# Second attention's row scores by way of a line in DRAM, in a two-layer graph kernel

## The chip, the cores and the metric

The kernel runs on one core of a Trainium2 chip. The metric is the device time of one execution in microseconds. Before the change the median of three runs is 2951.56 us (2950.34 to 2952.9).

## The reference

The input is 64 graphs of 256 nodes with 256 features, and a 0/1 adjacency matrix for each. The first layer applies graph attention twice, adds the input, normalises, and ends with a feed-forward block. The second layer is an eight-head attention in which the adjacency picks the value matrix, with a feed-forward block of its own. The change is in the second of the two graph attentions:

```python
def _gat(h, adj, W, a, out_features):
    Wh = jnp.matmul(h, W)
    Wh1 = jnp.matmul(Wh, a[:out_features])
    Wh2 = jnp.matmul(Wh, a[out_features:])
    e = Wh1 + jnp.swapaxes(Wh2, 1, 2)
    e = jax.nn.leaky_relu(e, negative_slope=ALPHA)
    scores = jnp.where(adj > 0, e, NEG)
    att = jax.nn.softmax(scores, axis=1)
    return jnp.matmul(att, Wh)
...
h = _gat(x, adj, W1, a1, Fout)
h = _gat(h, adj, W2, a2, W2.shape[1])
```

Each score is the sum of a number of one node and a number of the other. So a tile of scores needs one of the two vectors down the partitions (a column) and the other along the free axis, the same in all partitions (the rows).

## The kernel before, in words

Two graphs make a group; there are 32 groups. A group's 512 nodes are four blocks of 128 (T = 4). After a start that is written out by hand for groups 0 and 1, the kernel works in turns (`turn`, L1275). In turn u it carries three groups at once: Y = u through the second layer, X = u + 1 through the first layer's feed-forward block, and Z = u + 2 through the two graph attentions. The 30 turns u = 0 to 29 have a Z; the last two have none.

Within a turn the order on TensorE, SP, VectorE and ScalarE is the order of the program text (`manual_schedule`, L1323 to L1325). GpSimd's order, and the way in which one turn's VectorE and ScalarE work interleaves with the next turn's, is left to a planner. Engines wait for each other through semaphores.

The part of a turn around the change, in program order:

- `first_sums(z, ...)` (L1530, L1535): TensorE multiplies the first attention's weights with the values, and ScalarE copies the result to `hp` (L841), 260 columns wide, of which 258 are written. The first 256 columns are the second attention's values, column F = 256 the number for the rows, column F + 1 the number for the columns.
- `hidden_seven` (L908) for Y: the first matmul of the second layer's feed-forward block in seven products of half size instead of eight ("2a" to "4b", the letter names one half of the outputs). VectorE and ScalarE gather the products in `h` (L947, L950), and ScalarE applies the activation (L956). Laid between these steps is X's norm: moments (L865), GpSimd's power (L877), ScalarE's and GpSimd's normalising (L894, L891), the affine step for Y (L903, L906), and `normed_features` (L712), which transposes 32x32 blocks on VectorE (L717) and moves them to their places with 12 DMAs on SP (L726, `hT<-yt`) and 4 copies on GpSimd.
- `second_scores(z)` (L1588): `score_rows` (L777) makes the rows. For each of the four blocks TensorE transposes column F of `hp`, spread over 128 columns, into a PSUM bank (L781), so that every partition holds the same line. `Softmax.raw` (L797, L799) adds the column number to it on ScalarE, 256 elements at a time; `leaky` (L807) follows on VectorE, then `exp` (L810), `masks` (L814), the reciprocal (L818) and `scaled` (L830).
- `HiddenOut` (L997) for Y: the feed-forward block's second matmul, again in seven products. Product 1 reads `h`. Product 5 reads the quarter sum s1 = a21 + a22, which `out.sums(1, 2)` makes on VectorE (L1013, tile `eq`); `out.add` adds the products to `y` (L1035). Then TensorE applies the second attention's weights (`second_sums`, L1206, tile `ygp`).

```python
            second_scores(z)
            out = HiddenOut(y_, 1, y, h1, w2s, out_sums(y_, 1))
            out.product(1)
            out.sums(1, 2)
            Z["m"].scores(0)
            out.add(1)
            out.product(5)
            Z["m"].scores(1)
```

On SP's queue, ahead of the 12 moves, stand the store of the group before (L1243) and the load of the next group's rows `y` (L441); behind them come the 8 loads of the next adjacency (L449), and the moves for Y's and X's other norms (L737). The pool tag `es` has two buffers; `node_sums` (L1131) and `reciprocals` (L1149) take them. PSUM has a tag `g` with six banks, which the rows share with the products.

Of the kernel before, what the change touches and what calls it, by code (L numbers as in the profile page):

```python
# [9 lines left out]
F32 = mybir.dt.float32  # L10
# [6 lines left out]
P = 128  # L17
# [368 lines left out]
def narrow_path(  # L386
# [13 lines left out]
    nc = tc.nc  # L400
    B, N, F = x.shape
# [7 lines left out]
    T = G * NB  # L409
    TN = G * N  # L410
# [6 lines left out]
    const = ctx.enter_context(tc.tile_pool(name="const", bufs=1))  # L417
    io = ctx.enter_context(tc.tile_pool(name="io", bufs=2))
    work = ctx.enter_context(tc.tile_pool(name="work", bufs=2))
    psum = ctx.enter_context(tc.tile_pool(name="psum", bufs=1, space=PSUM))  # L420
    ctx.enter_context(nc.allow_non_contiguous_dma(reason="vectors, once"))

    def bank(name):
        return psum.tile([P, 512], F32, tag="g", name=name, bufs=6)
# [258 lines left out]
    rows = work.tile([P, T, 2 * F], F32, tag="v", name="rows", bufs=1)  # L683
# [93 lines left out]
    def score_rows(u, l, wh, c):  # L777

        rows = bank(f"rows{u}_{l}")
        for t in range(T):  # L780
            nc.tensor.transpose(rows[:, t * P:(t + 1) * P],  # L781
                                wh[:, t, c:c + 1].to_broadcast([P, P]), ident)
        return rows

    class Softmax:
# [46 lines left out]
    def gat_first(u, s, xp, hp=None, blocks=range(T)):  # L832
        if hp is None:
            hp = work.tile([P, T, WX], F32, tag="wh", name=f"hp{u}")
        for t in blocks:
            b, i = divmod(t, NB)
            ps = bank(f"hpp{u}_{t}")
            for j in range(NB):
                nc.tensor.matmul(ps[:, :WH], s[:, b * NB + j, i * P:(i + 1) * P],  # L839
                                 xp[:, b * NB + j, :WH], start=(j == 0), stop=(j == NB - 1))  # L840
            nc.scalar.copy(hp[:, t, :WH], ps[:, :WH])  # L841
        return hp
# [199 lines left out]
    def out_sums(u, l):  # L1042
        two = [work.tile([P, HPB, NB * N], F32, tag=t, name=f"{t}q{u}_{l}") for t in ("e", "ea")]
        return [t[:, :, i * N:(i + 1) * N] for t in two for i in range(2)]
# [136 lines left out]
        d = g[z]  # L1181
        d["xp"] = projected(z, d["xT"], blocks, d.get("xp"))

    def first_scores(z):
        d = g[z]
        d["m"] = Softmax(z, 0, d["xp"], score_rows(z, 0, d["xp"], F + 2), F + 3)

    def second_scores(z):
        d = g[z]
        d["m"] = Softmax(z, 1, d["hp"], score_rows(z, 1, d["hp"], F), F + 1)  # L1190

    def first_softmax(z):
        first_scores(z)
        g[z]["m"].all()
        g[z]["m"].scaled(WH)

    def second_softmax(z):
        second_scores(z)
        g[z]["m"].all()
        g[z]["m"].scaled(F)  # L1200

    def first_sums(z, blocks=range(T)):
        d = g[z]
        d["hp"] = gat_first(z, d["m"].s, d["xp"], None if blocks[0] == 0 else d["hp"], blocks)
# [70 lines left out]
    def turn(y_, x_, z, rest=None):  # L1275
        Y, X, Z = (g.get(u) for u in (y_, x_, z))
        hT, y = Y["hT"], Y["y"]
        quads = [(b, m) for b in range(G) for m in range(KB)]
        p = Projections(y_, hT)
# [45 lines left out]
        with order:  # L1325
# [151 lines left out]
            if Z:  # L1477
                first_scores(z)
# [54 lines left out]
                n = moments(x_, 1, X["y"], range(NB))  # L1533
            if Z:
                first_sums(z, range(T // 2, T))  # L1535
            if X:
                out.product(4)
            tt = work.tile([P, HPB, NB * N], F32, tag="e", name=f"tt{y_}_1")
# [39 lines left out]
            if y_ >= NG - 2:  # L1578
# [5 lines left out]
                else:  # L1584
                    for _ in pieces:
                        pass
                return
            second_scores(z)  # L1588
            out = HiddenOut(y_, 1, y, h1, w2s, out_sums(y_, 1))
            out.product(1)  # L1590
            out.sums(1, 2)
# [26 lines left out]
    with tc.manual_schedule(engines={getattr(mybir.EngineType, n) for n in  # L1618
# [21 lines left out]
        turn_a = early_adjacency_of(0, 1)  # L1640
        turn_a()
        first_scores(0)
        shift_products(ps, wf1, range(4, FB), lb1)
        shift_added(ps, range(FB), bf1)
# [13 lines left out]
        scaled_rows(wqk, *pqk)  # L1658
        nc.vector.tensor_tensor(wv[:, :, 1, :], wv[:, :, 1, :], wv[:, :, 0, :], ALU.subtract)
        second_scores(0)  # L1660
        turn_b.append(early_adjacency_of(1, 1))
        spread(a["m"])
# [115 lines left out]
    with tc.manual_schedule(engines={mybir.EngineType.PE, mybir.EngineType.SP}):  # L1778
        for u in range(NG):
            turn(u, u + 1, u + 2, second_half)  # L1780


    c = work.tile([P, 4], F32, tag="mv", name="checks")
# [13 lines left out]
@with_exitstack  # L1797
def tile_gat_layer__then__relational_attention_layer(ctx: ExitStack, tc: tile.TileContext, *args):
    nc = tc.nc
    keep = ctx.enter_context(tc.tile_pool(name="keep", bufs=1))  # L1800
    bad = keep.tile([1, 1], I32, name="bad")
    narrow_path(tc, *args, bad)
    with tc.If(nc.values_load(bad[0:1, 0:1], min_val=0, max_val=P) > 0):
        general_path(tc, *args)
# [30 lines left out]
```

## Time and profile before

| | |
|---|---|
| Median of three runs | 2951.56 us |
| The profiled execution's own time | 2950.62 us |
| Its span, first to last instruction | 2949.0 us |
| TensorE matmul busy | 2921.7 us (99%) |
| VectorE busy | 2611.3 us (89%) |
| ScalarE busy | 1897.2 us (64%) |
| GpSimd busy | 625.6 us (21%) |
| Row transposes for the second attention (L781, `rows<-ident,hp`) | 128 of 273 ns (median) |
| ScalarE's additions on them (L799, `s<-rows,hp`) | 128 of 478 ns (median) |
| Granted TensorE clock | 0.998 |

PE is TensorE's matmul, PEld its weight load, which overlaps matmuls; DVE is VectorE, ACT ScalarE, POOL GpSimd, SPq the queue of SyncE that issues DMAs. In a timeline the columns are the start in us from the span's start, the duration in us, engine, line, operation, output and inputs, shapes and the number of instructions merged into one line. A bracket tells how long the engine was idle before it and what ended that. Matmuls overlap, so the distance between the starts tells more than the durations.

### The profile page before, as it was taken

The numbers are of one execution on the slowest core, as the hardware profiler recorded it, in microseconds if no ns is written. First come the engines' busy times: TensorE is split into PE (matmuls) and PEld (weight loads), VectorE is DVE, ScalarE is ACT, GpSimd is POOL, SyncE is SP. The second block draws the span as 40 slices with busy tenths as digits, with TensorE's granted clock in tenths as the row PEclk, the third lists the DMA queues.
The fourth block names the chain that finished last, engine by engine and source line by source line (L and its number), as shares of the span: only waits on it lengthen the run. The fifth ranks groups of instructions, "written<-read, shape, count | busy, mean of one in ns | idle before, by whom it ended". The sixth has DMA issues, their size and how long they took to land.

```text
span 2949.0 us, 58651 instructions
## 1 busy us (share of the span) xinstructions
PE 2921.7 (99%) x22206; PEld 2505.9 (85%) x22206; DVE 2611.3 (89%) x5028; ACT 1897.2 (64%) x3983; POOL 625.6 (21%) x931
## 2 busy tenths in 40 slices
PE   9999999999999999999999999999999999999997
PEld 7788888888888888888888888888888888888876
DVE  5889899989899889999898998899998989988887
ACT  5566666676676666666766766766667667667652
POOL 3312221122121122221221211222212212112211
PEclk9999999999999999999999999999999999999999
DMA  5011111111111111111111111111111111111000
GB/s 152 13 30 32 39 32 32 24 40 32 37 30 26 34 34 38 33 31 24 40 32 37 31 28 31 36 36 35 29 23 40 32 37 32 28 30 33 18 8 16
DMA packets 408020, 99.27 MB, mean 34 GB/s; under 512 B 357834, under 2 KB 407220, under 8 KB 407732
## 3 DMA queue, kind: packets, MB, share of 16 engines
q1 hardware_dynamic: 406332, 94.13, 14.8%
q8 instruction: 178, 2.92, 0.4%
q0 software_dynamic: 1056, 1.05, 0.1%
q14 instruction: 110, 0.90, 0.1%
q10 hardware_dynamic: 344, 0.28, 0.0%
HBM read 56.78 MB, written 16.78 MB: 25 GB/s over the span
## 4 chain that ended last, share of the span: by engine, by line
PE 97%; DVE 2%; ACT 1%; DMA 0%; issue 0%; POOL 0%; DVEq 0%; POOLq 0%; ACTq 0%
PE yf L1027 27%; PE h1a L938 15%; PE h1b L938 11%; PE po L1143 8%; PE v L1094 6%; PE qk L1094 6%; PE sp L1115 4%; PE hpp L839 4%; PE ygp L850 4%; PE xpp L772 4%; PE yop L850 4%; PE zo L1146 2%; PE rows L781 1%; DMA first<-in_adj_dram 0%; DVE st L865 0%
## 5 line engine op out<-in xcount | busy, mean ns | idle before, releaser
L1124 ACT ACTIVATE e<-sp 128x512 f32<-128x512 f32 x512 | 271.0, 611 | 71.2 <-issue 43.7
L1128 DVE TENSOR_TENSOR ea<-e,aT 128x1024 f32<-128x1024 f32 x256 | 311.1, 1217 | 1.6 <-ACT e L1124 1.6
L894 ACT ACTIVATE y<-y,nm,rs 128x256 f32<-128x256 f32 x442 | 235.1, 592 | 64.0 <-DVE nm L884 63.2
L947 DVE TENSOR_TENSOR h<-h1a,h 128x512 f32<-128x512 f32 x293 | 197.5, 682 | 81.7 <-PE h1a L938 78.5
L950 ACT COPY h<-h1b 128x512 f32<-128x512 f32 x293 | 175.2, 599 | 124.6 <-PE h1b L938 122.8
L956 ACT ACTIVATE h<-h,cols 128x256 f32<-128x256 f32 x512 | 221.9, 502 | 35.7 <-DVE h L947 31.5
L734 POOL COPY hT<-yt 32x256 f32<-32x256 f32 x244 | 211.3, 866 | 144.8 <-DVE yt L717 132.1
L1081 ACT COPY qk<-qk 128x512 f32<-128x512 f32 x128 | 74.3, 580 | 237.4 <-PE qk L1094 236.6
L865 DVE BATCH_NORM_STATS2 st<-y 128x6 f32<-128x256 f32 x512 | 208.7, 409 | 5.7
L876 POOL TENSOR_SCALAR rs<-mv 128x4 f32<-128x4 f32 (+1 forms) x134 | 41.7, 312 | 805.1 <-DVE mv L866 438.5
L1035 DVE TENSOR_TENSOR y<-yf,y 128x256 f32<-128x256 f32 x448 | 185.9, 415 | 29.8 <-PE yf L1027 29.8
L956 ACT ACTIVATE h<-h1a,cols 128x256 f32<-128x256 f32 x256 | 102.6, 465 | 131.9 <-PE h1a L938 131.9
L1156 POOL TENSOR_TENSOR low<-low,rq 128x16 f32<-128x16 f32 x64 | 13.9, 217 | 811.6 <-DVE rq L1155 811.6
L906 DVE TENSOR_TENSOR y<-y,rb 128x1024 f32<-128x1024 f32 x126 | 163.2, 1295 | 2.2
L1133 DVE TENSOR_TENSOR es<-e 128x1024 f32<-128x1024 f32 x128 | 156.0, 1219 | 0.0
L903 DVE TENSOR_TENSOR y<-y,rg 128x1024 f32<-128x1024 f32 x126 | 153.0, 1214 | 0.0
L877 POOL TENSOR_TENSOR rs<-rs,mhalf 128x4 f32<-128x4 f32 (+1 forms) x134 | 139.5, 1041 | 8.3
L1115 PE MATMUL sp<-qk 32*128 32x256 f32 x2048 | 138.4, 394 | 0.0
L938 PE MATMUL h1a<-tt,wf 128*128 128x256 f32 x512 | 137.7, 392 | 0.0
L1143 PE MATMUL po<-e,v 128*32 128x256 f32 x2048 | 135.5, 382 | 0.0
L1143 PE MATMUL po<-ea,v 128*32 128x256 f32 x2048 | 134.5, 379 | 0.0
L717 DVE STREAM_TRANSPOSE yt<-y 128x256 f32<-128x256 f32 x364 | 128.2, 407 | 0.9 <-ACT y L894 0.7
(288 smaller groups left out, 7738.4 us busy)
## 6 DMA issues: line engine op xcount, KB each, us to landing
hT<-yt SPq DMA_DIRECT2D x666, 32.0 KB, 1.8
y<-in_x_dram SPq DMA_DIRECT2D x32, 512.0 KB, 4.1
xq<-in_x_dram SPq DMA_DIRECT2D x240, 64.0 KB, 2.3
aq<-in_adj_dram SPq DMA_DIRECT2D x240, 64.0 KB, 2.3
out_dram<-y SPq DMA_DIRECT2D x30, 512.0 KB
wf<-in_L_gnn_w_ff_dram SPq DMA_DIRECT2D x2, 1024.0 KB, 7.8
w<-in_L_gnn_W_dram SPq DMA_DIRECT2D x2, 1024.0 KB
first<-in_adj_dram POOLq DMA_DIRECT2D x2, 512.0 KB, 9.0
```

The lines of the kernel that those rows point to most:

```text
L734: nc.gpsimd.tensor_copy(to, at)
L850: nc.tensor.matmul(ps[:, i * F:(i + 1) * F], lhs(t, k), rhs(b, k), start=(k == 0), stop=(k == n - 1))
L865: nc.vector.bn_stats(st[:, t, :], y[:, t, :])
L894: mark["normed"] = nc.scalar.activation(y[:, t, :], y[:, t, :], AF.Identity, bias=nm[:, t:t + 1], scale=rs[:, t:t + 1])
L938: nc.tensor.matmul(ps[:, i * N:(i + 1) * N], w_[:, f * P:(f + 1) * P], m, start=first and i == 0, stop=True, skip_group_check=True)
L956: nc.scalar.activation(y, y if ps is None else ps[:, i * N:(i + 1) * N], func, bias=bi[:, f:f + 1])
L1027: nc.tensor.matmul(s.ps[n][:, i * F2:(i + 1) * F2], a[:, k, i * P:(i + 1) * P], w_[:, k, :], start=n in (1, 2, 5) and i == 0 and k == 0, s ...
L1094: nc.tensor.matmul(ps[:, i * N:(i + 1) * N], l, r, start=n in (1, 2, 5) and i == 0, stop=True, skip_group_check=True)
L1115: nc.tensor.matmul(ps[a][:, j * N:(j + 1) * N], k_[hp, m, j0:j0 + P], q[hp, m, b * N:(b + 1) * N], start=True, stop=True)
L1124: nc.scalar.activation(e[:, a, :], ps[a], AF.Exp, scale=isd)
L1128: nc.vector.tensor_tensor(ea[:, a:a + 2, :], e[:, a:a + 2, :], ab[:, None, :].to_broadcast([P, 2, NB * N]), ALU.mult)
L1143: nc.tensor.matmul(po[hp, m * N:(m + 1) * N], vs[:, hp], w[:, a, j * N:(j + 1) * N], start=(n == 0), stop=(n == len(terms) - 1))
```

## The change

The rows of the second attention are no longer transposed by TensorE. A new function `line_rows` is called in the turn as soon as `first_sums` has been issued. It has SP write column F of `hp` to a line of 512 numbers in DRAM, and then read the line into all 128 partitions of an SBUF tile (tag `es`). `second_scores` takes this tile instead of calling `score_rows`. `score_rows` stays for the first attention of all groups, and for the second of groups 0 and 1.

```diff
+    dram = ctx.enter_context(tc.tile_pool(name="dram", bufs=2, space=bass.MemoryType.DRAM))
...
+    def line_rows(u, l, wh, c):
+
+        line = dram.tile([T, P], F32, tag="line", name=f"line{u}_{l}")
+        rows = work.tile([P, TN], F32, tag="es", name=f"rows{u}_{l}")
+        nc.sync.dma_start(line.rearrange("t p -> p t"), wh[:, :, c])
+        nc.sync.dma_start(rows, bass.AP(tensor=line.tensor, offset=line.offset, ap=[[0, P], [1, TN]]))
+        return rows
...
-    def second_scores(z):
+    def second_scores(z, rows=None):
         d = g[z]
-        d["m"] = Softmax(z, 1, d["hp"], score_rows(z, 1, d["hp"], F), F + 1)
+        d["m"] = Softmax(z, 1, d["hp"], score_rows(z, 1, d["hp"], F) if rows is None else rows, F + 1)
...
             if Z:
                 first_sums(z, range(T // 2, T))
+                rows1 = line_rows(z, 1, Z["hp"], F)
...
-            second_scores(z)
+            second_scores(z, rows1)
```

`first_scores` gets the same optional argument; no call passes it.

More of the change, by code (lines that the diff above doesn't have):

```diff
@@ L1182, in project, with first_scores @@
         d["xp"] = projected(z, d["xT"], blocks, d.get("xp"))
-    def first_scores(z):
+    def first_scores(z, rows=None):
         d = g[z]
-        d["m"] = Softmax(z, 0, d["xp"], score_rows(z, 0, d["xp"], F + 2), F + 3)
-    def second_scores(z):
+        d["m"] = Softmax(z, 0, d["xp"], score_rows(z, 0, d["xp"], F + 2) if rows is None else rows, F + 3)
+    def second_scores(z, rows=None):
         d = g[z]
-        d["m"] = Softmax(z, 1, d["hp"], score_rows(z, 1, d["hp"], F), F + 1)
+        d["m"] = Softmax(z, 1, d["hp"], score_rows(z, 1, d["hp"], F) if rows is None else rows, F + 1)
     def first_softmax(z):
```

## The prediction

> **What bounds the kernel now.** I read the page first: TensorE's busy share and the chain that ended last.
>
> ```profile
> PE 2921.7 (99%) x22206; PEld 2505.9 (85%) x22206; DVE 2611.3 (89%) x5028; ACT 1897.2 (64%) x3983; POOL 625.6 (21%) x931
> PE 97%; DVE 2%; ACT 1%; DMA 0%; issue 0%; POOL 0%; DVEq 0%; POOLq 0%; ACTq 0%
> ```
>
> TensorE is on the path almost throughout. A turn (two graphs) takes 1511.74 - 1421.78 = 89.96 us by the starts of its second row transposes, and the later turns differ from that by 0.03 us at most; so I price one turn and multiply by 30, the number of turns that make second scores. Next, TensorE's timeline where the four transposes stand.
>
> ```profile
> 1420.05 1.89 PE L938 MATMUL h1a<-tt,w 128*128 128x256 f32 x8
> 1421.78 0.60 PE L781 MATMUL rows<-ident,hp 128*128 128x128 f32 x4
> 1422.21 1.95 PE L1027 MATMUL yf<-w,h 128*128 128x128 f32 x16
> 1424.00 1.95 PE L1027 MATMUL yf<-w2t,eq 128*128 128x128 f32 x16
> ```
>
> They hold TensorE from 1421.78 to 1422.21: 0.43 us, or 30 x 0.43 = 12.9 us in all. Behind them come product 1 (it reads `h`) and at 1424.00 product 5, which reads `eq`, the first of the quarter sums. So I looked at who makes `eq`: VectorE, ScalarE and TensorE's weight loads, each by its own timeline.
>
> ```profile
> 1419.22 3.30 ACT L956 ACTIVATE h<-h,cols 128x256 f32<-128x256 f32 x8 [1.04 <-DVE h L947]
> 1422.43 1.53 ACT L956 ACTIVATE h<-h1a,cols 128x256 f32<-128x256 f32 x4
> 1423.85 1.55 ACT L799 ACTIVATE s<-rows,hp 128x256 f32<-128x256 f32 x4
> ```
>
> ```profile
> 1418.55 1.24 DVE L947 TENSOR_TENSOR h<-h1a,h 128x512 f32<-128x512 f32 x2
> 1419.72 1.26 DVE L947 TENSOR_TENSOR h<-h1b,h 128x512 f32<-128x512 f32 x2
> 1422.56 1.23 DVE L1013 TENSOR_TENSOR eq<-h 128x1024 f32<-128x1024 f32 x1 [1.57 <-ACT h L956]
> ```
>
> ```profile
> 1423.67 0.30 PEld L1027 LDWEIGHTS yf<-w,h 128*128 128x128 f32 x2
> 1423.90 0.19 PEld L1027 LDWEIGHTS yf<-w2t,eq 128*128 128x128 f32 x1
> ```
>
> `eq` is done at 1422.56 + 1.23 = 1423.79, and product 5's first weights load at 1423.90, 0.11 us later. Is that slack, or a wait that just ended? The last matmul of the kernel gives the measure, since it is idle for 4.88 us until VectorE's `good` is there:
>
> ```profile
> 2942.64 0.16 DVE L1791 TENSOR_TENSOR good<-good 128x1 f32<-128x1 f32 x1
> 2942.91 0.11 PEld L1793 LDWEIGHTS goodp<-ones,good 128*1 128x1 f32 x2 [4.88 <-issue]
> ```
>
> 2942.64 + 0.16 = 2942.80 to 2942.91: also 0.11 us. Product 5 stands at the distance of a wait in full. The trace's nanoseconds agree: in 29 of the 30 turns the distance is 114 to 116 ns (125 in the first), while the step from the weight load before varies from 113 to 124 ns where it is 112 within a product. **TensorE already arrives at product 5 a few nanoseconds before `eq` does.** The transposes fill a wait.
>
> **What the Trainium skill says.** (1) "Perfetto Trace Analysis", section "Sequencer-only Instruction", says that a profiled window begins when all semaphores are satisfied, so the wait itself isn't shown. The trace agrees: product 5's semaphore instruction is recorded at 51 ns in each turn, and at 51 ns too before the last matmul, after a wait of 4.88 us. This is why no view lists this wait. (2) "TensorE: Matmul & The Clock Gate", "Part 4: PE-mode transpose", gives some 275 ns to a 128x128 transpose in a kernel; here 273 ns, but overlapped to 0.11 each. (3) "DMA: Bandwidth & Descriptors", "Two DMAs through the same engine are not ordered", has the issuing engine wait for the first DMA's semaphore before it issues one that reads its bytes; so SP will stand. No such pair is in the trace of before. (4) Same page, "Specifications" and "Latency and other measured facts": under 512 B the transfer is a read-modify-write, and HBM access takes 0.2 us on average. The trace has no payload of 4 B to compare.
>
> **The change part by part.** *Removed:* 4 transposes per turn, 0.43 us of TensorE. They come after all that `eq` waits for. Backwards from `eq`: ScalarE's 8 activations from 1419.22, which waited for VectorE's add at 1418.55; VectorE is busy with norm, affine and block transposes from 1414.48, when GpSimd's `rs` came; that came from moments at 1412.30, behind an add that waited for product 1a, done at 1411.58. No step of it is a row transpose or reads one. From 1a to product 5 it takes 1423.90 - 1411.58 = 12.32 us, and TensorE's own work over the same stretch now takes 12.32 - 0.43 = 11.89. So TensorE will do product 1 at 1421.78 and then wait 0.43 us for `eq`. Gain per turn: 0.00. Bounds: a weight load that waits itself follows VectorE by 0.05 us (`y` of L1035), which would gain 0.06; behind four semaphore instructions (the first hidden product, after ScalarE's `e`) it follows by 0.18, which would lose 0.07. Over 30 turns -1.8 to +2.1 us; I take 0.
>
> *The PSUM bank* that the rows held is free earlier. Product 1 and the banks after it don't wait for a bank now: nothing.
>
> *Scores from SBUF:* the four L799 take 478 ns each from PSUM. Nearest rows: L956 takes 465 from PSUM and 502 from SBUF, L894 592 with two pointer operands. So -0.01 to +0.11 us each; I take +0.04, 0.16 in all. Cover: the first leaky step on VectorE starts at 1424.96, behind the quarter sums, while its two scores end at 1424.68 (0.28 spare); the second at 1425.89 against 1425.40 (0.49). Even +0.44 is covered; uncovered, it would cost 30 x 0.16 = 4.8 us.
>
> *Two DMAs on SP per turn.* SP's timeline:
>
> ```profile
> 1409.23 0.39 SPq L441 DMA_DIRECT2D y<-in_x_dram  x1
> 1418.68 8.72 SPq L726 DMA_DIRECT2D hT<-yt  x12
> 1429.03 5.32 SPq L449 DMA_DIRECT2D aq<-in_adj_dram  x8
> ```
>
> and the landing times of the DMA view:
>
> ```profile
> hT<-yt SPq DMA_DIRECT2D x666, 32.0 KB, 1.8
> y<-in_x_dram SPq DMA_DIRECT2D x32, 512.0 KB, 4.1
> ```
>
> `hp` is complete at 1408.48, so the line is issued behind the load of `y`, at 1409.7, and moves when that has landed, 1409.23 + 4.1 = 1413.3. It is 512 elements, 32 for each of 16 engines. Low bound 1.8 us (a 32 KB move); high bound 32 x 0.2 = 6.4 us, an estimate from (4). I take 2.5: landed at 1415.8, at the latest 1419.7. SP stands until then. Queued behind it are the 12 moves `hT<-yt`, which can't start before 1418.68 anyway. The rows, 256 KB, take 1.8 to 4.1 us; with 4.1 they are there at 1419.9, at the latest 1423.8. Needed: 1423.85, when ScalarE has finished L956. In the late case the moves slip by 0.4 (issue) + 1.0 = 1.4 us, the last landing at 1427.4 + 1.8 + 1.4 = 1430.6; their first reader, VectorE's L1062 for the next turn, is at 1431.14. The adjacency load behind them moves to 1429.0 + 0 because it waits for ScalarE until 1429.03, or 1.2 at worst, and is read half a turn later. Cost on the path: 0.
>
> *The `es` buffer* that the rows take had its last reader in `sums(3)`, some 20 us before; the next taker comes in the next turn, after the scores. Nothing. *GpSimd* gets no instruction.
>
> Sum: -12.9 us of TensorE work, +12.9 us of waiting. The profiled execution has a span of 2949.0 and took 2950.6 us; 2950.6 + 0 = 2950.6. The median of the three runs is 0.9 above it, so I forecast 2951.5.
>
> **The rivals.** *B, the plain reading: TensorE is 99% busy, so its work counts in full.* 2951.5 - 12.9 = 2938.6. For it: the chain shows no wait at product 5. Against: `eq` cannot be read before 1423.79, whatever TensorE leaves out. It would need `eq` to be earlier by 0.43 us.
>
> *C, slower: the line is slow to land.* Place: SP's wait ahead of the rows, then ScalarE's L799. It decides from 0.2 us per element. At 0.25 (8 us) the line lands at 1421.3, the rows at 1425.4, 1.55 us late; 0.28 is spare, so VectorE's leaky step, and behind it all the adds and quarter sums that products 6, 3 and 7 wait for, come 1.3 us late: 30 x 1.3 = 38 us, 2990. For it: no 4-byte payload has been measured. Against: the 1 KB packets of the load of `y` take 46 ns each in the trace, and 128 B packets 13.
>
> *D, the planner's seam.* VectorE's order is fixed within a turn, but the next turn's L1062 slips in ahead of this turn's last softmax steps (1431.14, before the reciprocal). TensorE's read of the scaled `hp` has 0.18 us to spare (scaled at 1432.59, weights loaded at 1432.82, less 0.05 us of signal). One more such step of 0.33 us ahead costs 30 x 0.15 = 4.5 us, two 14: 2956 to 2966. For it: other durations in the plan. Against: what makes room there, the reciprocal's own wait, is unchanged.
>
> **How the numbers follow.** A (as forecast) 0.80, its own range 2948.5 to 2955; B 0.05; C 0.07; D 0.08, of which 0.02 inside 0.2%. A measurement of this kernel can tell about 0.2%, 5.9 us, from no change. Faster 0.05, same 0.80 + 0.02 = 0.82, slower 0.07 + 0.06 = 0.13. The range takes in A with its bounds and D's first step: 2947 to 2960.
>
> **What would show it.** Right: a turn still 89.96 us; TensorE's busy time some 12 us lower; before product 5's weights a new gap of 0.4 us; the load still 0.11 us after `eq`; `rows` landed before 1420 of that turn. Wrong: a turn of 89.5 us (B); ScalarE waiting for a DMA at L799 and SP's moves after 1418.7 (C); more VectorE steps between the masks and the reciprocal (D). The forecast falls if `eq` comes earlier, relative to product 1a, than now.

## The result, and the profile after

The changed kernel takes 2956.25 us (median), the kernel before 2952.01 beside it: a ratio of 1.0017, 95% interval 1.0009 to 1.0024. That is +4.2 us by the medians and about 5 by the ratio: within the forecast's range and near 0.2%, but with 22 runs of each it is told from no change. It is not the nothing that was forecast.

The profiled execution after has a span of 2952.6 us and took 2954.2. First the page of the changed kernel: busy time by engine, the chain that ended last, and product 5's group (out<-in, count, busy us and mean ns, idle time before it and what ended that).

```profile
PE 2916.7 (99%) x22086; PEld 2492.0 (84%) x22086; DVE 2605.4 (88%) x5028; ACT 1904.0 (64%) x3983; POOL 622.5 (21%) x931
...
PE 85%; DVE 8%; ACT 4%; POOL 1%; issue 1%; DMA 1%; SPq 0%; DVEq 0%; POOLq 0%; ACTq 0%
...
L1036 PE MATMUL yf<-w2t,eq 128*128 128x128 f32 x992 | 122.9, 277 | 6.3 <-DVE eq L1022 6.3
```

120 transposes are gone and TensorE is still on the path, but the chain has moved: 85% PE in place of 97%, because it now leaves TensorE at each product 5 and goes through `eq`.

The waits of the changed kernel (engine, line, what it waited for: us in total, times, longest):

```profile
ACT s L808 <- DMA rows<-line: 11.3, 19, 1.4
PEld yf L1036 <- PE yf L1036: 11.2, 30, 0.4
...
DVE tq L1071 <- DMA hT<-yt: 0.3, 1, 0.3
```

The second is the hidden wait of the prediction, come to light: 30 times, 11.2 / 30 = 0.37 us on the weight load. (Matmuls here start 0.11 us apart but are drawn with 277 ns each, so the last one ahead of the gap covers part of it: the matmul row of the page shows only 6.3 / 30 = 0.21.) The first is new and was forecast at nothing: ScalarE stands at the scores for `rows` in 19 turns. The third is small and new too: once, VectorE waits for the last of SP's moves, which were pushed back.

A median would hide what that costs, so I measured every turn by the start of product 5's first weight load: 29 full turns in each trace. Before: median 89.964 us, and only the first turn over 90; sum 2609.20. After: median 89.975, but ten turns are longer by more than 0.1, up to 90.91; sum 2613.49. The difference, 4.29 us, is the size of the loss. (It comes from one execution of each kernel. These two differ by 2954.2 - 2950.6 = 3.6 us as a whole; the stretches ahead of and behind the 29 turns vary as well.)

One turn that was held, in the changed kernel: ScalarE's, VectorE's, TensorE's and the weight loads' timelines (start, duration, in brackets the idle time before and what ended it).

```profile
974.00 1.53 ACT L965 ACTIVATE h<-h1a,cols 128x256 f32<-128x256 f32 x4
976.61 1.71 ACT L808 ACTIVATE s<-rows,hp 128x256 f32<-128x256 f32 x4 [1.07 <-DMA rows<-line]
```

```profile
974.13 1.23 DVE L1022 TENSOR_TENSOR eq<-h 128x1024 f32<-128x1024 f32 x1 [1.58 <-ACT h L965]
977.55 0.69 DVE L816 SCALAR_TENSOR_TENSOR s<-s 128x512 f32<-128x512 f32 x1 [0.94 <-ACT s L808]
```

```profile
973.34 1.95 PE L1036 MATMUL yf<-w,h 128*128 128x128 f32 x16
975.50 2.02 PE L1036 MATMUL yf<-w2t,eq 128*128 128x128 f32 x16 [0.21 <-DVE eq L1022]
```

```profile
975.47 1.86 PEld L1036 LDWEIGHTS yf<-w2t,eq 128*128 128x128 f32 x16 [0.37 <-PE yf L1036]
```

Read down: `eq` is done at 974.13 + 1.23 = 975.36 and the weights follow at 975.47, 0.11 us later, just as before. ScalarE, free at 975.53, gets its rows only at 976.61; VectorE's leaky step waits 0.94 us for it, and from these weights to those of the next turn it takes 90.61 us, 0.64 over the median. In the seven turns that ScalarE's wait held most, its start stood 0.71 to 1.43 us after product 5's weights, and the turn grew by 0.22 to 0.94: each time 0.49 or 0.50 less. Undelayed, the scores start 0.04 us ahead of those weights, so 0.53 us of delay are covered.

SP's queue in the same turn, then the landings from its DMA view (count, KB, median us from issue to landing; none is given for `rows`):

```profile
960.98 0.39 SPq L442 DMA_DIRECT2D y<-in_x_dram  x1
961.46 0.46 SPq L790 DMA_DIRECT2D line<-hp  x1
971.17 0.34 SPq L791 DMA_DIRECT2D rows<-line  x1
971.62 8.34 SPq L727 DMA_DIRECT2D hT<-yt  x12
```

```profile
y<-in_x_dram SPq DMA_DIRECT2D x32, 512.0 KB, 4.9
...
line<-hp SPq DMA_DIRECT2D x30, 2.0 KB, 9.3
```

2 KB take 9.3 us to land, 512 KB take 4.9. (The trace gives a landing for 7 of the 30 lines.) SP stands 971.17 - 961.46 = 9.71 us between the two DMAs here, 8.3 to 11.1 over all 30 turns, median 9.5. From the issue of the rows to ScalarE's first use it is 976.61 - 971.17 = 5.44 us here, 3.9 to 5.7 in the turns where ScalarE waited, median 5.0. The DMA packets in the trace tell where the 9.3 us go: in the turn shown the line's 4-byte packets stand behind the load's 1 KB packets and are over 3.2 us after the line's issue. Some 6 us pass between the last packet and the landing, and no data packet is drawn in them.

### The profile page after: what moved, and what is told of

It is laid out like the page before. It is cut to its first block, busy times and chain, and to the rows that moved or that the text cites. A ratio compares the mean times of both kernels' runs of the same rounds, so it can differ in the third digit from the quotient of the medians.

```text
span 2952.6 us, 58500 instructions
## 1 busy us (share of the span) xinstructions
PE 2916.7 (99%) x22086; PEld 2492.0 (84%) x22086; DVE 2605.4 (88%) x5028; ACT 1904.0 (64%) x3983; POOL 622.5 (21%) x931
## 4 chain that ended last, share of the span: by engine, by line
PE 85%; DVE 8%; ACT 4%; POOL 1%; issue 1%; DMA 1%; SPq 0%; DVEq 0%; POOLq 0%; ACTq 0%
PE yf L1036 24%; PE h1a L947 9%; PE h1b L947 8%; PE po L1152 8%; PE v L1103 6%; PE qk L1103 6%; PE sp L1124 4%; PE hpp L848 4%; PE ygp L859 4%; PE xpp L773 4%; PE yop L859 4%; ACT h L965 3%; PE zo L1155 2%; DVE y L915 1%; DVE y L912 1%; DVE eq L1022 1%
## 5 line engine op out<-in xcount | busy, mean ns | idle before, releaser
L1036 PE MATMUL yf<-w2t,eq 128*128 128x128 f32 x992 | 122.9, 277 | 6.3 <-DVE eq L1022 6.3
```

Source lines behind the costliest of these rows:

```text
L1036: nc.tensor.matmul(s.ps[n][:, i * F2:(i + 1) * F2], a[:, k, i * P:(i + 1) * P], w_[:, k, :], start=n in (1, 2, 5) and i == 0 and k == 0, s ...
```

## The experiments

**The theories.** 1, mine after the result: the transposes filled a wait (gain 0), and the whole loss is `rows` coming late. 2: the loss comes from the extra DMAs and from SP's moves being pushed back behind the rows. 3: the scores' additions cost more from SBUF. 4, the plain reading: the transposes are worth 12.9 us and something of 17 us eats that gain. Each number below is a median with its ratio to the kernel before and the interval; "turn" is min / median / max of the 29 turns.

**e1: both DMAs stay, the scores read transposed rows again.** This keeps the traffic and SP's stand, and removes the dependence. (VectorE's order from the planner is that of the kernel before; in the changed kernel, e2, e3 and e11 some steps behind the reciprocal stand in another order. The turns of e2, e3 and e11 will show that this costs nothing.)

```diff
-            second_scores(z, rows1)
+            second_scores(z)
```

> The transposes are back and feed the scores; the line and the rows are still written and read by DMA, and nothing reads the rows tile. Theory 1 (the rows land too late for ScalarE, and only that costs): as before, 2952.0 us, ratio 1.000, turns of 89.97 us without exception. Theory 2 (SP's queue and the DMA traffic cost by themselves, through the moves that they push back): as the changed kernel, about 2956, ratio 1.0017, some turns of 90.3 to 90.9. Theory 3 (scores read from SBUF, or the planner's order): 2952.0, ratio 1.000, too.

Measured: 2951.69, 1.0001 (0.9992 to 1.0011); turn 89.961 / 89.964 / 90.63, sum 2609.83 (before: 2609.20). The first turn is long, as it is before, and one in the middle is 0.67 over the median; the other 27 lie within 0.02 us. SP's queue in an ordinary turn of e1, then VectorE in the long one:

```profile
789.99 0.67 SPq L790 DMA_DIRECT2D line<-hp  x1
800.31 0.34 SPq L791 DMA_DIRECT2D rows<-line  x1
```

```profile
1981.56 0.42 DVE L1071 TENSOR_TENSOR tq<-hT 128x256 f32<-128x256 f32 x1 [0.71 <-DMA hT<-yt]
```

SP stands 10.3 us here and the moves behind come about as late as in the changed kernel (they begin 1.1 us later than before, by the medians of both), yet the ten long turns are not there. So theory 2 falls as the account of the loss, but a small part of it stands: the one long turn of e1 is a turn in which VectorE waited 0.71 us for a pushed-back move. In the changed kernel the same wait came once, 0.26 us long, in a turn that grew by 0.12 though its scores started only 0.30 us late, which is covered.

**e2: no rows at all.** The second attention's row part is left out: the additions read a constant tile in SBUF. No transpose, no DMA.

```diff
-                rows1 = line_rows(z, 1, Z["hp"], F)
+                rows1 = wvf[:, 0]
```

> The rows are left out: no transposes, no DMAs, the second attention's scores add a constant weight tile in SBUF instead of the row numbers. Theory 1, with the wait for the quarter sum hiding the transposes: 2952.0 us, ratio 1.000, turns of 89.97 us. The plain reading, that TensorE's work counts in full: 2939, ratio 0.9956, turns of 89.53. Theory 3 (reading the rows from SBUF is what costs): 2956, ratio 1.0017.

Measured: 2951.3, 0.9996 (0.9987 to 1.0006); turn 89.956 / 89.963 / 89.97, sum 2608.95. TensorE's timeline at the place of the former transposes, in e2, and the wait:

```profile
1421.72 1.95 PE L1036 MATMUL yf<-w,h 128*128 128x128 f32 x16
1423.87 2.02 PE L1036 MATMUL yf<-w2t,eq 128*128 128x128 f32 x16 [0.20 <-DVE eq L1022]
```

```profile
PEld yf L1036 <- PE yf L1036: 10.9, 30, 0.4
```

Product 1 is followed by product 5 after 2.15 us, where it was 1.79 (1422.21 to 1424.00): TensorE gets there earlier and stands. By the turn nothing is won. With the rows free of charge the change would have been worth nothing: theories 3 and 4 fall, and so does rival B.

**e3: the line ahead of the load of `y`.** I held that the line queues behind the 512 KB load.

```diff
         nc.sync.dma_start(line.rearrange("t p -> p t"), wh[:, :, c])
+        if u + 1 < NG:
+            load_rows(u + 1)
         nc.sync.dma_start(rows, bass.AP(...))
...
-            if z + 1 < NG:
+            if z + 1 < NG and not Z:
```

> SP writes the line ahead of the load of y, and issues that load while the line is on its way. The same DMAs, only in another order. Theory 1: the line is issued 1 us earlier and no longer moves behind 512 KB, so that it lands some 3 us earlier and the rows are there before ScalarE asks; 2952.0 us, ratio 1.000, all turns 89.97. Theory 2 and theory 3: as the changed kernel, 2956, ratio 1.0017.

Measured: 2950.89, 0.9997 (0.9986 to 1.0008); every full turn at most 89.97. SP's queue in one turn:

```profile
957.12 0.39 SPq L789 DMA_DIRECT2D line<-hp  x1
966.50 0.34 SPq L793 DMA_DIRECT2D rows<-line  x1
```

The loss is gone, but not for the reason I gave: SP stands 9.38 us here, 9.5 by the median, as in the changed kernel. The line's packets do come earlier, most of them 0.9 to 1.3 us after the issue in place of 2.7 to 3.2, but the landing does not follow. Only the issue is earlier, by 1.35 us. The line is slow by itself. The load of `y`, now behind the line, lands 11.9 us after its issue in place of 4.9; no turn waited for it.

**e4 to e7: is the hidden 0.43 us still to be had?** Product 5 waits for `eq`, and ahead of `eq` VectorE adds the affine's second half (1.46 us). The edit makes that addition later, once the `h1` adds are done. It goes on four kernels: before (e4), e2 (e5), e3 (e6) and the changed one (e7). e5 leaves out the row part as e2 does.

```diff
-                affine(y, rg3, rb3)
+                times(y, rg3)
...
-                second("7a 7b sa sb 3a da 3b db 4a 4b")
+                second("7a 7b sa sb 3a da 3b db")
+                plus(y, rb3)
+                second("4a 4b")
```

> The kernel before, with only the affine step moved (adding rb3 on VectorE goes behind the last add of hidden products). If the quarter sum and TensorE's own work meet at product 5 within nanoseconds, an earlier sum alone brings only these: 2951.2 us, ratio 0.9995 to 1.000, turns of 89.96. If the move itself were what gained in the run without rows: 2940, ratio 0.996.

> As the run without rows, and VectorE's second affine step for Y (adding rb3) is moved from ahead of the block transposes to behind the last add of hidden products, into the 1.57 us in which VectorE waits for ScalarE. If the quarter sum gates product 5, it comes 0.45 us earlier (GpSimd's normalising, done at 1417.71 in the turn shown, sets the transposes then), and the 0.43 us of the transposes come out: turns of 89.53 to 89.6, 2939 to 2941 us, ratio 0.9957 to 0.9965. If something else holds the turn: 2952, ratio 1.000.

> The changed kernel with the line ahead of the load of y, and with the affine step moved. Theory 1: rows are in time in nearly all turns, and the transposes' 0.43 us come out: ratio 0.9960 to 0.9970, 2940 to 2943 us, turns of 89.55. If the rows are late again because ScalarE asks 0.43 us sooner: 0.997 to 1.000.

> The changed kernel with the affine step moved and the line where the change has it. Theory 1: ScalarE asks 0.43 us sooner, so by the lateness of the rows in the changed kernel's trace some 20 of 30 turns are held, 11 us in all, which eats what comes out: ratio 0.9990 to 1.0005, about 2951. If the rows were not what holds it: 0.9962, as without rows.

| | Median us | Ratio (95%) | Turn min / median / max | Sum of turns |
|---|---|---|---|---|
| e4 | 2950.88 | 0.9996 (0.9986 to 1.0006) | 89.96, all alike | 2608.91 |
| e5 | 2944.0 | 0.9962 (0.9949 to 0.9975) | 89.517 / 89.523 / 89.62 | 2596.26 |
| e6 | 2937.24 | 0.9949 (0.9937 to 0.9962) | 89.518 / 89.524 / 90.14 | 2597.7 |
| e7 | 2955.17 | 1.0003 (0.9995 to 1.0011) | 89.523 / 90.312 / 91.18 | 2616.39 |

In e4 `eq` is early: VectorE's and the weight loads' timelines in one turn.

```profile
1430.44 1.22 DVE L1013 TENSOR_TENSOR eq<-h 128x1024 f32<-128x1024 f32 x1
```

```profile
1432.35 1.75 PEld L1027 LDWEIGHTS yf<-w2t,eq 128*128 128x128 f32 x15
```

It is done at 1430.44 + 1.22 = 1431.66, 0.69 us ahead of product 5's weights in place of 0.11, and the turn is as long as before. e4 against e5 is the test of the prediction's main step: with the transposes in place an earlier `eq` is worth nothing, without them it gives 89.963 - 89.523 = 0.44 us per turn, the transposes' 0.43. (e5's and e6's medians differ by more than their turns, and e6's is better than I expected: by its turns it gains 2609.20 - 2597.7 = 11.5 us. The stretch ahead of the first mark varies from 163 to 174 us between profiled executions of all kernels, so I compare turns.) e7 pays the gain back and more than I expected, 2616.39 - 2596.26 = 20.1 us over e5 for some 11: ScalarE's wait for `rows`, first of e6, then of e7.

```profile
ACT s L810 <- DMA rows<-line: 5.6, 8, 1.2
```

```profile
ACT s L808 <- DMA rows<-line: 36.1, 28, 2.3
```

TensorE comes earlier, the line does not, and 28 turns wait in place of 8.

**Why is the line slow?** Four runs. **e8** keeps one quarter of the line: 128 numbers in one row of 512 B, which serves for all four blocks (three quarters of the rows are left out). **e9** makes the line a tile in SBUF, written by four DMAs. **e10** puts each of the 512 numbers 512 B from the next; the rows aren't read (the row part is left out). **e11** spreads the line over 16 rows of 512 B with 32 numbers in each, by four DMAs.

```diff
 e8
+        nc.sync.dma_start(line[0:1].rearrange("t p -> p t"), wh[:, 0:1, c])
 e9
+        for t in range(T):
+            nc.sync.dma_start(line[0:1, t * P:(t + 1) * P], wh[:, t, c:c + 1])
+        nc.sync.dma_start(rows, line[0:1, None, :].to_broadcast([1, P, TN]))
 e10
+        line = dram.tile([T, P, 128], F32, ...)
+        nc.sync.dma_start(line[:, :, 0].rearrange("t p -> p t"), wh[:, :, c])
 e11
+        line = dram.tile([T * Q, P], F32, ...)
+        for q in range(Q):
+            nc.sync.dma_start(bass.AP(..., offset=line.offset + q * P, ap=[[1, 32], [Q * P, T]]),
+                              wh[q * 32:(q + 1) * 32, :, c])
+        nc.sync.dma_start(rows, bass.AP(..., ap=[[0, P], [P, T * Q], [1, 32]]))
```

> Of the row numbers only the first block's 128 are written to the line, and they are read four times over: three quarters of the rows are left out. What it tells is when the line is complete. If each 4-byte write takes its turn at DRAM: some 8 us of acknowledging become 2, the line is complete 3 to 4 us after its issue. If it is one fixed delay: 9 us again.

> The changed kernel with the line in one partition of an SBUF tile in place of DRAM: four DMAs of 128 elements write it, and one DMA reads it into all partitions. If it is the writes to DRAM that are slow to be acknowledged, the line is complete 2 to 4 us after its issue, the rows come in time, and the time is that of before: 2951.4, ratio 1.000. If 4-byte elements are slow wherever they go: 9 us again and ratio 1.0015 to 1.003.

> As the run without rows (the scores add a constant tile, the row part is left out), but the 512 numbers are still written to DRAM, each 512 bytes from the next, and nobody waits for them. What it tells is when the write is complete. If the delay comes from many small writes to the same 512 bytes: 3 to 4 us from issue in place of 9.3. If each small write is slow by itself: 9 us again, or more.

> The changed kernel with the line laid out in 16 rows of DRAM of 512 bytes that hold 32 numbers each, in place of 4 rows with 128; the write takes four DMAs of 32 partitions, the read takes pieces of 128 bytes. If writes to the same 512 bytes are acknowledged one after the other, some 45 to 50 ns apart, a row takes 1.5 us instead of 6: the line is complete 4 to 5.5 us after its last issue, ScalarE never waits for the rows, turns are 89.97 us and the ratio is 1.000. If only the number of elements counts: 9 us, and 1.0017 or more with the longer issue.

The DMA views of e8, e9, e10 and e11 in turn (count, KB, median us to landing):

```profile
line<-hp SPq DMA_DIRECT2D x30, 0.5 KB, 9.2
```

```profile
rows<-line SPq DMA_DIRECT2D x30, 256.0 KB, 11.5
...
line<-hp SPq DMA_DIRECT2D x120, 0.5 KB, 3.9
```

```profile
line<-hp SPq DMA_DIRECT2D x30, 2.0 KB, 3.8
```

```profile
rows<-line SPq DMA_DIRECT2D x30, 256.0 KB, 4.8
...
line<-hp SPq DMA_DIRECT2D x120, 0.5 KB, 5.9
```

A quarter of the numbers takes as long (9.2 against 9.3), so the number of elements is not the price, nor is an engine's share of them. Put 512 B apart, all 512 land in 3.8 us, so it is no fixed delay either. With 32 to a row of 512 B they take 5.9, with 128 to a row 9.2; e8's DMA and each of e11's carry the same 128 numbers, so the size of the DMA is not it. So the price lies in how many small writes fall close together: (9.3 - 3.8) / 128 = 43 ns for each that shares a row, an estimate, and rows side by side cost no more than one. 3.8 + 32 x 0.043 = 5.2 comes near e11's 5.9. (All these have the load of `y` ahead of them. The last turn has none: there e10's line lands in 1.8 us, and SP's stand in the changed kernel puts the packed one at 8.4, which makes (8.4 - 1.8) / 128 = 52 ns.) Whether the stretch that counts is 512 B or somewhat less, these runs don't tell: it must be over 128 B, since e11's numbers lie in runs of 128 B and still gain.

The times: e8 3090.73 (one run, 2950.74 beside it) and e9 3018.57, 1.0237 (1.0220 to 1.0255). I expected e9 to be free of loss. Its write is quick as I thought; the read that hands one partition's line to 128 takes 11.5 us, and ScalarE waits 76.7 us in 29 turns. In e8 ScalarE waits 141.2 us in 30 turns, at most 6.5: its read fetches the same 512 B over and over. Why those two reads are slow I did not take apart. e10: 2950.52 (one run). e11: 2952.56, 0.9997 (0.9990 to 1.0004); turn 89.959 / 89.967 / 90.25, sum 2609.31. (In its one long turn GpSimd's power came late, as in the same turn of e10, which reads no rows.) ScalarE never waits for `rows` in e11: **the loss is gone when the numbers are spaced.** The spaced line also takes four DMAs in place of one and is read in pieces of 128 B. But it is the earlier landing that ends the wait: from the line's first issue to the issue of the rows it takes 7.4 us in place of 9.5 (medians), and the read 4.8 in place of some 5.0.

**e12: e11's line in e6.**

> The spaced line together with the line ahead of the load of y and the affine step moved. Nothing should hold a turn: all turns 89.52 us, 2937 to 2940 us, ratio 0.9945 to 0.9962, and no turn of 89.8 or 90.1 as the run with the packed line showed.

Measured: 2938.86 (six runs), 0.9949 (0.9933 to 0.9965), turn 89.517 / 89.523 / 89.63, sum 2596.27. TensorE's timeline:

```profile
1416.22 1.95 PE L1040 MATMUL yf<-w,h 128*128 128x128 f32 x16
1418.01 1.95 PE L1040 MATMUL yf<-w2t,eq 128*128 128x128 f32 x16
```

No bracket at product 5: 1.79 us from product to product, as before the change, without the transposes and without a wait. Against e6 the median is not better, but no turn is held by `rows`. It is 2952.86 - 2938.86 = 14 us faster than the kernel before beside it.

## Why the prediction was right and where it was wrong

- **Transposes fill a wait, gain 0: right.** e2 wins nothing with TensorE relieved, and e4/e5 show the 0.44 us to be there as soon as `eq` is earlier. The Trainium skill, "Perfetto Trace Analysis", section "Sequencer-only Instruction", says that a semaphore wait lies outside the recorded window, and the 51 ns agree. But that is not why no view listed the wait before, as the prediction has it: a wait also shows as the idle time ahead of the next instruction, as the 11.2 us of after do. Before, by the prediction's reading, the transposes left only a few nanoseconds of it. What gave it away was the fixed 0.11 us from `eq` to the weights, not a row of any view.
- **"I take 2.5: landed at 1415.8": wrong, the first of two terms that failed in "Cost on the path: 0".** The landing came 9.3 us after the issue: 1409.7 + 9.3 = 1419.0, 3.2 us after the forecast and 0.7 ahead of the late bound of 1419.7. (In five turns SP stood 10.2 to 11.1 us, past that bound too.) That the line moves behind the load of `y` was right: its last packet ends 0.2 us after the load's last. What the sum lacked is the time from the last packet to the landing: 6.1 us (median of the seven turns that give a landing), and 0.5 in e10. The bound's reason, 0.2 us per element of an engine, was wrong: e8 has a quarter of the elements and lands as late. "DMA: Bandwidth & Descriptors", section "Specifications", does say that under 512 B the transfer is a read-modify-write; the runs put a price beside small writes, some 43 to 52 ns for each into the same row, as if one after another. That the read-modify-write is the reason no run shows.
- **"The rows take 1.8 to 4.1 us": too low, the second.** They took 3.9 to 5.7 where ScalarE waited, over 4.1 in 17 of these 19 turns. 1419.0 + 5.0 = 1424.0, with 5.7 it is 1424.7, against the limit of 1423.85: the limit was right, and two terms together crossed it by a little in most turns. My "late case" did put both at their bounds and came to 1423.8, 0.05 us short of the limit; but its 4.1 was no bound, only the median of another transfer, the load of `y`. Neither term crosses it alone: the line as measured with rows of 4.1 makes 1419.0 + 4.1 = 1423.1, the line as forecast with the slowest rows 1415.8 + 5.7 = 1421.5.
- **SP's moves, "cost 0": nearly.** In the late case their last landing was to stay ahead of its first reader. It did in all turns of the changed kernel but one, where VectorE waited 0.26 us.
- **The cover of 0.28 us: low.** The turns show 0.53, so seven of the 19 waiting turns grew by nothing.
- **Rival C had the place** (SP's wait, then ScalarE at L799, then the leaky step), not the cause (a price per element of an engine, against e8) and not the size: 4.3 us in place of 38. I gave it only one size, the one where every turn is late by 1.3 us; a sum that just crosses its limit costs part of the turns a part of that. **B** falls by e2. **D** did not occur: one step stands between the masks and the reciprocal as before; behind the reciprocal the order did change, in e2 too, and turns of e2, and those after that aren't held, stay flat.
- **Scores from SBUF: right.** The four additions take 1.71 us in the timeline shown, 1.55 in that of before: +0.16 in all, +0.04 each, as forecast. They start further apart; the single one is 494 ns against 478. Covered, by e2 and e3.
- **TensorE's busy time "some 12 us lower":** 5.0 lower, since only 6.3 of the 11.2 us of waiting are drawn as idle on the matmul row; the weight loads, 2505.9 to 2492.0, show the removed work better.

Left open: one more of the ten long turns grew by 0.11 where ScalarE's delay explains 0.03, with SP's moves as late as in the turn where VectorE waited for them; that they are its cause is not shown. What moves the start of the kernel by up to 10 us between executions was not looked into further.

## What to carry to other kernels

A producer-to-matmul distance that stayed within 2 ns in 29 of 30 turns was a wait here, though no view listed one: where you find such a distance, price the removal of work ahead of it at nothing, and ask what makes the producer earlier, since here the two edits pay only together. When two unknown transfers stand in series, a median of some other transfer is no upper bound for either; where the sum of the bounds comes within 0.05 us of the limit, call it uncovered, and price a crossing at its partial size too. A column that went to DRAM as single numbers wanted its numbers spread out, not packed: 32 to a row in place of 128 took the line from 9.3 to 5.9 us, and away went the loss.

## What the hardware showed that I had not expected

512 writes of 4 B into 2 KB of DRAM land in 9.3 us, 128 of them into one 512 B in 9.2, the 512 of them 512 B apart in 3.8, though each packet shows only 9 ns in the trace; between the last packet and the landing lie 6.1 us for the packed line and 0.5 for the one spread out. Spreading one SBUF partition's 2 KB to 128 partitions takes 11.5 us, from 16 spaced pieces in DRAM 4.8. Four of ScalarE's additions take 1.71 us from SBUF where they took 1.55 from PSUM.
